# The last batch's output projection: weight sums and residual loads ahead, products between the small ones, results by one VectorE operation per 128 columns

## The chip, the cores and the metric

The kernel runs on one core of a Trainium2 chip, in one launch. The metric is the device time in microseconds; before the change three runs gave a median of 3935.7 (3933.7 to 3947.99).

## The reference

The input is 8 images of 512 channels and 32 x 32 = 1024 positions, in float32. Two layers follow, each an attention block on a normalised input with a residual. The change lies in the end of the second layer, of which this is the core (gn is a group norm without weights; the 4-d shapes are left out):

```python
def layer1(x, w_q, w_k, w_v, w_head, in_gamma, in_beta, w_proj, b_proj):
    n = gn(x)                                            # 8 x 512 x 1024
    q, k, v = (heads(w @ n) for w in (w_q, w_k, w_v))    # 8 heads of 64
    attn = einsum('bhdq,bhdT->bhqT', q, k) * 64 ** -0.5
    attn = einsum('gh,bhqT->bgqT', w_head, attn)         # mixes the heads
    attn = softmax(attn, axis=-1)
    mean, var = moments(attn, axes=(-2, -1))             # one pair for each head
    attn = (attn - mean) / sqrt(var + 1e-5) * in_gamma + in_beta
    out = einsum('bhqT,bhdT->bhqd', attn, v)
    out = out.reshape(b, 1024, 512)                      # mixes heads with tokens
    return x + (out @ w_proj.T + b_proj).transpose(0, 2, 1)
```

Since the mean of a softmax over its matrix is known, the normalisation of a head g is a scale A[g] and an offset; the offset goes through the sum of v, and through w_proj, to a constant for each output channel and head. The kernel writes `a.A` for the scales and `a.cv` for the offsets before the projection.

## The kernel before

Each image is worked on in turn; `b` counts them, and the last is b = 7. In the second layer, the order of every engine's instructions is the order of the program text (`tc.manual_schedule`): no planner moves anything. SyncE issues the large DMAs in the same order, and an issue that waits holds back those behind it.

For each image a loop over 8 blocks of queries (`p`) with 4 steps each forms scores (`scores`), brings them to ScalarE and by DMA into another grouping (`regroup`, tile `re`), mixes the heads (`mix`, exponentials on ScalarE), transposes on VectorE (`flip`), takes the moments (`moments`) and multiplies with v (`values`, `leave`). Two blocks make a chunk `n` of 128 channels of the attention's output, kept unnormalised in the tile `q` (`out_view`). `totals(n)` makes the row sums with small matmuls (L1780, L1782), takes their reciprocal (L1784), stores it (`zd`, L1790); `broadcast` loads it back spread over the partitions (`rzb`, L1802), and `divide(n)` multiplies the chunk by it (L1829). For the first three chunks these run in the course of the loop, on GpSimd; for the last chunk they come at the end, on SyncE's queue and VectorE.

In the first seven images the output projection takes seven products of half-size matrices. The last one has nothing behind it to overlap with, and goes its own way, in `out1_last`. It computes four output chunks `oc` of 128 channels, each from four input chunks `n` and in two halves `f` of 512 columns (a head owns 128 columns, so half f has the heads 4f to 4f + 3). `products(oc, blocks)` does the given input chunks of output chunk oc, and remembers which are done; chunks 0, 1 and 2 have a two-bank PSUM tile each, chunk 3 has two single banks, `halves`. A product of 512 columns in float32 shows as two matmul records in the trace. The scale A and the offset are applied to the product, not to the input: `instance` sums the squares (tile `isb`), `instance_end` multiplies with ones to add over the partitions (L1854), and works out A and cv with operations of 128 x 8, among them `rsqrt`. Four small matmuls (L1592) multiply cv with the sum of the weights over the input chunks (`wsum`, L1583 and L1585); with the bias they give `off`, which ScalarE adds to the residual x, 128 columns at a time (L1603). `check` counts row sums out of range, and `set_flag` turns that into a flag by a matmul (L1964); the flag is read at the program's end, and another path would run again if it were set.

At the end of the last image, the program's order is: the last `values`; `totals`, `broadcast` and `instance` of the last chunk; then `rest`. `rest` loads the residual, and then, for oc of 0 to 2, finishes the products of the input chunks 0 to 2 (chunk 0 is already complete in these, chunk 1 lacks one), with the weight sums, `instance_end`, `divide` and `check` behind oc 0, the small matmuls and ScalarE's additions behind oc 1, and the flag behind oc 2. After that come the products that need the divided chunk, all of chunk 3, and for each half a multiplication by A, an addition of the residual (L1623, L1628) and the store (L1629).

Of the kernel before, what the change touches and what calls it, by code (L numbers as in the profile page):

```python
# [9 lines left out]
F32 = mybir.dt.float32  # L10
I32 = mybir.dt.int32
AF = mybir.ActivationFunctionType
ALU = mybir.AluOpType
# [5 lines left out]
P = 128  # L19
# [448 lines left out]
def tile_two_attention_layers(  # L468
# [19 lines left out]
    nc = tc.nc  # L488
    B, C, T = x_d.shape
    H = w_head.shape[0]  # L490
    D = C // H
    NCC = C // P
    NT = T // P
    FB = 512
    NFB = T // FB
# [10 lines left out]
    def column(name, src):  # L506
        t = const.tile([P, src.shape[0] // P], F32, tag=name, name=name)
        nc.gpsimd.dma_start(out=t, in_=src.rearrange("(c p) -> p c", p=P))
        return t
# [13 lines left out]
    pb1 = column("pb1", b_proj)  # L523
# [142 lines left out]
    ys = const_tile("ys", [P, B, NCC])  # L666
# [34 lines left out]
    with ExitStack() as l0:  # L701
# [4 lines left out]
        zpool = l0.enter_context(tc.tile_pool(name="zpool", bufs=2))  # L706
# [572 lines left out]
    with ExitStack() as l1:  # L1279
# [5 lines left out]
        zpool = l1.enter_context(tc.tile_pool(name="zpool1", bufs=1))  # L1285
# [4 lines left out]
        NCH = NT // 2  # L1290

        def acc_psum(nm):
            return ps_a.tile([P, FB], F32, tag="a", name=nm)
# [10 lines left out]
        NF = 5  # L1304
        re_t = repool.tile([P, NF + 4, 2, FB], F32, tag="re", name="re")
# [62 lines left out]
        class Projection:  # L1368
# [10 lines left out]
            def products(self, m):  # L1379
                w = w_t[self.key]  # L1380
                left, right = {
                    1: (0, self.b11), 2: (1, self.b21), 3: (6, self.b22), 4: (2, self.t[:, 3]),
                    5: (3, self.t[:, 0]), 6: (4, self.t[:, 1]), 7: (5, self.t[:, 2]),
                }[m]
                if m == 2:
                    self.ps[2] = self.ps.pop(1)
                else:
                    self.ps[m] = m_psum(f"{self.nm}_{m}")
                for i in range(2):
                    for k in range(2):  # L1390
                        nc.tensor.matmul(  # L1391
                            self.ps[m][:, i], w[:, left, k * HC + i * P : k * HC + i * P + P],
                            right[:, k], start=(k == 0 and m != 2), stop=(k == 1),
                            skip_group_check=True,
                        )
# [114 lines left out]
        def out_view(b):  # L1510


            return qo_t[b].rearrange("p (n two) a t -> p n (two a t)", two=2)
# [36 lines left out]
        def out1_last(a):  # L1550


            b = a.b
            w = w_t["p", b]
            tiles, done = {}, set()

            def products(oc, blocks):
                blocks = [n for n in blocks if (oc, n) not in done]
                done.update((oc, n) for n in blocks)
                if oc not in tiles:  # L1560
                    tiles[oc] = m_psum(f"pp1_{b}_{oc}")
                for f in range(NFB):
                    for n in blocks:
                        nc.tensor.matmul(  # L1564
                            tiles[oc][:, f], w[:, n, ts(oc, P)], out_view(b)[:, n, ts(f, FB)],
                            start=(n == 0), stop=(n == NCH - 1),
                        )

            last = NCH - 1

            def rest():

                x = rawpool.tile([P, NCC, T], F32, tag="raw", name="xs_last")
                for oc in range(NCC):
                    nc.sync.dma_start(out=x[:, oc], in_=x1_d[b][ts(oc, P), :])
                wsum = epool.tile([P, 2 * T], F32, tag="e", name="wsum")[:, :C]
                ys = etpool.tile([P, NCC, NFB, FB], F32, tag="et", name="ys_last")
                small = acc_psum("small_last")
                off = stat.tile([P, NCC, H], F32, tag="off", name="off", bufs=1)
                for oc in range(3):  # L1580
                    products(oc, range(last))
                    if oc == 0:
                        nc.vector.tensor_add(wsum, w[:, 0], w[:, 1])  # L1583
                        for n in range(2, NCH):
                            nc.vector.tensor_add(wsum, wsum, w[:, n])  # L1585
                        a.instance_end(small)
                        a.divide(last)
                        a.check()
                    if oc == 1:
                        pc = small[:, H : H + NCC * H]  # L1590
                        for o in range(NCC):
                            nc.tensor.matmul(  # L1592
                                pc[:, o * H : o * H + H], wsum[:, ts(o, P)], a.cv,
                                start=True, stop=True,
                            )
                        nc.vector.tensor_add(
                            off, pc.rearrange("p (c g) -> p c g", g=H),
                            pb1.unsqueeze(2).to_broadcast([P, NCC, H]),
                        )
                        for o in range(NCC):  # L1600
                            for g in range(H):
                                xg = x[:, o, ts(g, P)]
                                nc.scalar.activation(  # L1603
                                    xg, xg, AF.Identity, bias=off[:, o, g : g + 1]
                                )
                set_flag(small)
                halves = [acc_psum(f"pp1_last_{f}") for f in range(NFB)]
                h = FB // P
                for oc in range(NCC):
                    if oc < last:  # L1610
                        products(oc, [last])
                    for f in range(NFB):
                        if oc < last:
                            ps = tiles[oc][:, f]
                        else:
                            ps = halves[f]
                            for n in range(NCH):
                                nc.tensor.matmul(  # L1618
                                    ps, w[:, n, ts(oc, P)], out_view(b)[:, n, ts(f, FB)],
                                    start=(n == 0), stop=(n == NCH - 1),  # L1620
                                )
                        y = ys[:, oc, f]
                        nc.vector.tensor_mul(  # L1623
                            y.rearrange("p (g t) -> p g t", t=P),
                            ps.rearrange("p (g t) -> p g t", t=P),
                            a.A[:, f * h : f * h + h].unsqueeze(2).to_broadcast([P, h, P]),
                        )
                        nc.vector.tensor_add(y, x[:, oc, ts(f, FB)], y)  # L1628
                        nc.sync.dma_start(out=out_d[b, ts(oc, P), ts(f, FB)], in_=y)  # L1629

            return products, rest

        class Attention1:
            def __init__(self, b):
# [169 lines left out]
                    in_=self.zd[t].rearrange("g i -> (g i)").partition_broadcast(D),  # L1804
                )

            def check(self):

                b = self.b
                zs = self.zs[:, :, :32]  # L1810
                junk = zpool.tile([P, T], F32, tag="rzb", name=f"junk_{b}")[
                    :64, : NCH * 32
                ].rearrange("p (n c) -> p n c", n=NCH)
                cnt = stat.tile([64, 2], F32, tag="cnt", name=f"cnt_{b}")
                nc.vector.tensor_scalar(
                    junk, zs, Z_MAX, 0.0, ALU.is_lt, ALU.add, accum_out=cnt[:, 0:1]
                )
                nc.vector.tensor_scalar(
                    junk, zs, 1.0 / RZ_MAX, 0.0, ALU.is_gt, ALU.add, accum_out=cnt[:, 1:2]
                )  # L1820
                nc.vector.tensor_add(cnt[:, 0:1], cnt[:, 0:1], cnt[:, 1:2])
                nc.vector.tensor_scalar(
                    chk[:64, 1, B * H + b : B * H + b + 1], cnt[:, 0:1],
                    -(2.0 ** 60), 2.0 ** 61 * NCH * 32, ALU.mult, ALU.add,
                )
# [151 lines left out]
        for b in range(B):  # L1977
            more = b + 1 < B
            a = Attention1(b)
# [32 lines left out]
            else:  # L2012
# [6 lines left out]
                out_products = []  # L2019
# [6 lines left out]
            last = NT - 1  # L2026
            a.sums(NCH - 1)
            if not more:
                a.values(last, 0, 2, 3)
                a.leave(last, 0)  # L2030
                out_products[0](0, [2])
                out_products[0](1, [0, 1])
                a.values(last, 1, 0, 1, 2, 3)
                a.leave(last, 1)
                a.totals(NCH - 1)
                a.broadcast(0)
                a.broadcast(1)
                a.instance()
                out_products[1]()
                continue  # L2040
# [83 lines left out]
```

## Time and profile before

| what | value |
|---|---|
| median of three runs | 3935.7 us (3933.7 to 3947.99) |
| the profiled execution: its time | 3948.04 us |
| its span, first to last instruction | 3946.2 us |
| mean granted TensorE clock | 0.998 |
| busy: TensorE (PE) | 3871.6 us, 98% |
| busy: VectorE (DVE) | 2736.6 us, 69% |
| busy: ScalarE (ACT) | 1966.8 us, 50% |
| last `values` matmul ends, by the chain | 3913.44 us |
| last product record ends, by the chain | 3939.83 us |
| last VectorE result ends | 3941.34 us |

A line of the timeline has the start in us from the span's start, the length, the engine, the line of the code, the operation, what it writes and reads with shapes, how many instructions are merged in it, and in brackets how long the engine idled before it and for what. The chain of waits goes back from the last instruction, at each step to what released it. DVE is VectorE, ACT is ScalarE, PE is TensorE, PEld its weight loads, SPq SyncE's queue.

### The profile page before, as it was taken

To read this page: it belongs to the slowest core of one execution; us is meant where nothing else is said; L and a number is where in the kernel's file an instruction comes from. 1 tells how busy PE (TensorE), PEld (TensorE's weight loads), DVE (VectorE), ACT (ScalarE), POOL (GpSimd) and SP (SyncE) were. 2 spreads that over 40 slices of the span, in tenths; PEclk is the share of its full clock that TensorE was granted. 3 is DMA by queue.
4 is the path that set the end of the run, shared out by engine and by line. 5 is a ranking of instruction groups with operands and counts; after the bars stand their busy time and mean duration, and the time that the engine had idled before them with its cause. 6 is when DMAs were issued, how large, how long until landed. Compare 5 with 4: busy or idle time off the path is not lost. (4 is left out here: it accounts for less than half of the span.)

```text
span 3946.2 us, 95344 instructions
## 1 busy us (share of the span) xinstructions
PE 3871.6 (98%) x41868; PEld 1822.3 (46%) x41868; DVE 2736.6 (69%) x3713; ACT 1966.8 (50%) x2400; POOL 207.4 (5%) x210
## 2 busy tenths in 40 slices
PE   8999999999999999999999999999999999999998
PEld 4353535344353535344554544545545545445454
DVE  4747476665758474756867958859768678678597
ACT  1726354453627172534725717528447257176275
POOL 0000000000000000000110100201101102002010
PEclk9999999999999999999999999999999999999999
DMA  3313131212121121216947839749559479297395
GB/s 120 120 53 116 49 116 43 84 35 77 55 75 66 64 73 52 87 46 168 221 135 190 230 97 229 191 128 239 167 149 228 142 177 223 97 227 204 114 228 146
DMA packets 249593, 519.09 MB, mean 132 GB/s; under 512 B 51024, under 2 KB 58192, under 8 KB 242512
## 3 DMA queue, kind: packets, MB, share of 16 engines
q1 hardware_dynamic: 241984, 500.08, 44.7%
q0 software_dynamic: 7184, 12.81, 1.6%
q8 instruction: 331, 5.42, 0.6%
q14 instruction: 94, 0.77, 0.1%
HBM read 197.16 MB, written 46.92 MB: 62 GB/s over the span
## 5 line engine op out<-in xcount | busy, mean ns | idle before, releaser
L1712 DVE STREAM_TRANSPOSE et<-e 128x2048 f32<-128x2048 f32 x256 | 589.5, 2303 | 133.5 <-ACT e L1697 132.5
L1742 PEld LDWEIGHTS a<-et,v 128*64 128x64 f32 x16384 | 506.4, 138 | 294.0 <-issue 268.5
L1726 DVE BATCH_NORM_STATS2 bn<-e 128x6 f32<-128x512 f32 x1024 | 635.0, 680 | 0.0
L1093 ACT ACTIVATE e<-s 128x1024 f32<-128x1024 f32 x512 | 497.1, 1026 | 232.8 <-PE s L1088 232.7
L1659 ACT COPY raw<-s 128x1024 f32<-128x1024 f32 x480 | 470.2, 1018 | 218.9 <-PE s L1647 192.5
L1697 ACT ACTIVATE e<-m 128x1024 f32<-128x1024 f32 x512 | 496.2, 1021 | 157.4 <-PE m L1684 55.1
L1742 PE MATMUL a<-et,v 128*64 128x64 f32 x16384 | 554.7, 224 | 8.7 <-issue 6.2
L1103 DVE TENSOR_TENSOR zacc<-zacc,e 128x1024 f32<-128x1024 f32 x384 | 468.8, 1221 | 124.6 <-ACT e L1093 100.5
L1647 PE MATMUL s<-k,q 64*64 64x512 f32 x4096 | 515.6, 606 | 6.9 <-DVE q L1506 3.2
L1088 PE MATMUL s<-q,k 64*64 64x512 f32 x4096 | 490.3, 594 | 2.3 <-ACT e L1093 2.3
L1116 PE MATMUL a<-e,v 64*64 64x512 f32 x4096 | 484.1, 589 | 0.0
L1684 PE MATMUL m<-re,wmix 32*32 32x512 f32 x8192 | 312.8, 599 | 17.8 <-DMA re<-raw 14.4
L1116 PEld LDWEIGHTS a<-e,v 64*64 64x64 f32 x4096 | 156.6, 133 | 282.8 <-issue 282.3
L1088 PEld LDWEIGHTS s<-q,k 64*64 64x64 f32 x4096 | 146.4, 133 | 284.2 <-issue 217.8
L1647 PEld LDWEIGHTS s<-k,q 64*64 64x64 f32 x4096 | 128.0, 132 | 222.5 <-issue 90.5
L1790 POOL DMA_DIRECT2D zd<-rz x96 | 52.3, 550 | 3390.0 <-DMA y<-x 1868.5
L1466 PE MATMUL pv<-wv,y 128*128 128x512 f32 x480 | 216.0, 603 | 0.0
L1758 ACT COPY q<-a 64x256 f32<-64x256 f32 x256 | 93.8, 367 | 136.4 <-PE a L1742 134.5
L1466 PEld LDWEIGHTS pv<-wv,y 128*128 128x128 f32 x480 | 89.3, 191 | 120.9 <-issue 107.5
L1684 PEld LDWEIGHTS m<-re,wmix 32*32 32x32 f32 x8192 | 69.3, 103 | 163.2 <-ACT raw L1659 71.7
L1472 DVE COPY v<-pv 128x512 f32<-128x512 f32 x30 | 20.7, 690 | 159.7 <-ACT v L1472 80.3
L906 PE MATMUL pv_p<-left_v,tmp 128*128 128x256 f32 x512 | 115.0, 380 | 3.3 <-DVE tmp L935 3.3
(318 smaller groups left out, 3859.5 us busy)
## 6 DMA issues: line engine op xcount, KB each, us to landing
re<-raw SPq DMA_DIRECT2D x1024, 256.0 KB
left_q<-left_q SPq DMA_DIRECT2D x17, 1792.0 KB
left_p<-left_p SPq DMA_DIRECT2D x17, 1792.0 KB
left_k<-left_k SPq DMA_DIRECT2D x10, 1792.0 KB
x<-in_x_dram SPq DMA_DIRECT2D x32, 512.0 KB
rzb<-zd SPq DMA_DIRECT2D x128, 128.0 KB
x<-x SPq DMA_DIRECT2D x64, 256.0 KB
y<-x SPq DMA_DIRECT2D x32, 512.0 KB
```

Source lines behind the costliest of these rows:

```text
L1088: nc.tensor.matmul(ps[c * D : c * D + D, m], k[r, hp, k0 : k0 + D], q[r, hp, ts(f, FB)], start=True, stop=True,)
L1093: nc.scalar.activation(e[i], ps, AF.Exp, scale=S0 * S0)
L1103: nc.vector.tensor_add(zacc[g], zacc[g], e[i])
L1116: nc.tensor.matmul(acc[g][a][m * D : m * D + D], v[rows, kc, ts(2 * hp + m, D)], e[i][rows, m], start=(kc == 0), stop=(kc == NG - 1),)
L1466: nc.tensor.matmul(ps[:, m], y_t[b][:, c, ts(2 * i + m, P)], w[:, c], start=(c == 0), stop=(c == NCC - 1),)
L1647: nc.tensor.matmul(ps[c * D : c * D + D, m], qo_t[b][r, p, hp, ts(c, D)], k_t[b][r, hp, ts(kh, FB)], start=True, stop=True,)
L1659: nc.scalar.copy(dst, ps)
L1684: nc.tensor.matmul(ps[a // 2][c * 32 : c * 32 + 32, a % 2].rearrange("p (r h k) -> p h r k", r=2, h=2), wmix[rows].rearrange("p g i -> p ( ...
L1697: nc.scalar.activation(e[:, :, 2 * h : 2 * h + 2].rearrange("p r a k -> p a r k"), ps[h].rearrange("p a (r k) -> p a r k", r=2), AF.Exp,)
L1712: nc.vector.transpose(self.et[p, u].rearrange("p kb (r st a) g q -> p st kb r (a g q)", r=2, st=2)[:, st], self.e[p, s].rearrange("p r a ( ...
L1726: nc.vector.bn_stats(self.bn[n][:, p % 2, s, a], e[:, :, a].rearrange("p r k -> p k r"))
L1742: nc.tensor.matmul(acc[two * D : two * D + D, s].rearrange("p (x q) -> p x q", q=4), v_t[b][:, kb, ts(g, D)], et[:, kb, :, g], start=(kb = ...
```

## The change

- The residual loads and the weight sums move out of `rest` into a new function `inputs`. It is called before the last `values` of the last query block: the loads go to SyncE's queue ahead of `zd` and `rzb`, the sums to VectorE ahead of the row sums' reciprocal.
- The missing products of chunk 1 go before the `isb` matmul, and those of chunk 2 between it and the small matmuls. Half 0 of chunk 3 is begun (three of its four input chunks) before the flag's matmul.
- `check` comes directly behind `instance_end`, and writes what it has no use for to a free part of the tile `re`, no longer to the buffer of `rzb`. `divide` comes behind `off`, and the 32 additions of ScalarE are written behind `set_flag`.
- The multiplication and the addition on 512 columns (two operations) become four operations on 128 columns, each with one column of A as its scalar.

```diff
-            def rest():
+            kept = []
+
+            def inputs():
                 x = rawpool.tile([P, NCC, T], F32, tag="raw", name="xs_last")
                 for oc in range(NCC):
                     nc.sync.dma_start(out=x[:, oc], in_=x1_d[b][ts(oc, P), :])
                 wsum = epool.tile([P, 2 * T], F32, tag="e", name="wsum")[:, :C]
+                nc.vector.tensor_add(wsum, w[:, 0], w[:, 1])
+                for n in range(2, NCH):
+                    nc.vector.tensor_add(wsum, wsum, w[:, n])
+                kept.extend((x, wsum))
+
+            def rest():
+                x, wsum = kept
                 ...
-                for oc in range(3):
-                    products(oc, range(last))
-                    if oc == 0:
-                        nc.vector.tensor_add(wsum, w[:, 0], w[:, 1])
-                        for n in range(2, NCH):
-                            nc.vector.tensor_add(wsum, wsum, w[:, n])
-                        a.instance_end(small)
-                        a.divide(last)
-                        a.check()
-                    if oc == 1:
-                        pc = small[:, H : H + NCC * H]
                 ...
+                products(1, range(last))
+                a.instance_end(small)
+                a.check(re_t[:64, NF + 3, 1, : NCH * 32])
+                products(2, range(last))
+                pc = small[:, H : H + NCC * H]
+                for o in range(NCC):
+                    nc.tensor.matmul(
+                        pc[:, o * H : o * H + H], wsum[:, ts(o, P)], a.cv,
+                        start=True, stop=True,
+                    )
+                nc.vector.tensor_add(
+                    off, pc.rearrange("p (c g) -> p c g", g=H),
+                    pb1.unsqueeze(2).to_broadcast([P, NCC, H]),
+                )
+                halves = []
+
+                def half(f, blocks):
+                    if f == len(halves):
+                        halves.append(acc_psum(f"pp1_last_{f}"))
+                    for n in blocks:
+                        nc.tensor.matmul(
+                            halves[f], w[:, n, ts(last, P)], out_view(b)[:, n, ts(f, FB)],
+                            start=(n == 0), stop=(n == NCH - 1),
+                        )
+
+                half(0, range(last))
+                a.divide(last)
                 set_flag(small)
+                for o in range(NCC):
+                    for g in range(H):
+                        xg = x[:, o, ts(g, P)]
+                        nc.scalar.activation(
+                            xg, xg, AF.Identity, bias=off[:, o, g : g + 1]
+                        )
                 ...
                         else:
+                            half(f, [last] if f == 0 else range(NCH))
                             ps = halves[f]
                 ...
-                        y = ys[:, oc, f]
-                        nc.vector.tensor_mul(
-                            y.rearrange("p (g t) -> p g t", t=P),
-                            ps.rearrange("p (g t) -> p g t", t=P),
-                            a.A[:, f * h : f * h + h].unsqueeze(2).to_broadcast([P, h, P]),
-                        )
-                        nc.vector.tensor_add(y, x[:, oc, ts(f, FB)], y)
-                        nc.sync.dma_start(out=out_d[b, ts(oc, P), ts(f, FB)], in_=y)
+                        for i in range(h):
+                            g = f * h + i
+                            nc.vector.scalar_tensor_tensor(
+                                ys[:, oc, f, ts(i, P)], ps[:, ts(i, P)], a.A[:, g : g + 1],
+                                x[:, oc, ts(g, P)], ALU.mult, ALU.add,
+                            )
+                        nc.sync.dma_start(out=out_d[b, ts(oc, P), ts(f, FB)], in_=ys[:, oc, f])
 ...
                 a.leave(last, 0)
                 out_products[0](0, [2])
                 out_products[0](1, [0, 1])
+                out_products[2]()
                 a.values(last, 1, 0, 1, 2, 3)
```

More of the change, by code (lines that the diff above doesn't have):

```diff
@@ L1579, in rest @@
                 off = stat.tile([P, NCC, H], F32, tag="off", name="off", bufs=1)
-                for oc in range(3):
-                    products(oc, range(last))
-                    if oc == 0:
-                        nc.vector.tensor_add(wsum, w[:, 0], w[:, 1])
-                        for n in range(2, NCH):
-                            nc.vector.tensor_add(wsum, wsum, w[:, n])
-                        a.instance_end(small)
-                        a.divide(last)
-                        a.check()
-                    if oc == 1:
-                        pc = small[:, H : H + NCC * H]
[L1591 to L1594, printed above, removed]
-                            )
-                        nc.vector.tensor_add(
-                            off, pc.rearrange("p (c g) -> p c g", g=H),
-                            pb1.unsqueeze(2).to_broadcast([P, NCC, H]),
-                        )
[L1600 to L1605, printed above, removed]
@@ L1606, in rest @@
-                set_flag(small)
-                halves = [acc_psum(f"pp1_last_{f}") for f in range(NFB)]
+                products(1, range(last))
[8 more added lines that the diff above has]
+                    )
@@ L1615, in rest @@
                         else:
+                            half(f, [last] if f == 0 else range(NCH))
                             ps = halves[f]
[L1617 to L1621, printed above, removed]
-                        y = ys[:, oc, f]
-                        nc.vector.tensor_mul(
-                            y.rearrange("p (g t) -> p g t", t=P),
-                            ps.rearrange("p (g t) -> p g t", t=P),
-                            a.A[:, f * h : f * h + h].unsqueeze(2).to_broadcast([P, h, P]),
-                        )
-                        nc.vector.tensor_add(y, x[:, oc, ts(f, FB)], y)
-                        nc.sync.dma_start(out=out_d[b, ts(oc, P), ts(f, FB)], in_=y)
-            return products, rest
+                        for i in range(h):
[5 more added lines that the diff above has]
+                        nc.sync.dma_start(out=out_d[b, ts(oc, P), ts(f, FB)], in_=ys[:, oc, f])
+            return products, rest, inputs
         class Attention1:
@@ L1805, in broadcast, with check @@
                 )
-            def check(self):
+            def check(self, place=None):
                 b = self.b
                 zs = self.zs[:, :, :32]
-                junk = zpool.tile([P, T], F32, tag="rzb", name=f"junk_{b}")[
-                    :64, : NCH * 32
-                ].rearrange("p (n c) -> p n c", n=NCH)
+                if place is None:
+                    place = zpool.tile([P, T], F32, tag="rzb", name=f"junk_{b}")[:64, : NCH * 32]
+                junk = place.rearrange("p (n c) -> p n c", n=NCH)
                 cnt = stat.tile([64, 2], F32, tag="cnt", name=f"cnt_{b}")
```

## The prediction

> **What bounds the kernel now.** The page comes first: TensorE (PE) is busy 98% of 3946.2 us, and the granted clock is full almost throughout. The edit touches only the end of the eighth batch, so I then read the chain that ended last, restricted to its last 47 us (columns: start, length, what).
>
> ```profile
> 3913.58 0.31 PE z L1782 x4
> ...
> 3916.19 0.69 DVE wsum L1583
> ...
> 3917.62 0.69 DVE wsum L1585
> 3918.31 0.09 DVE ivar L1856
> ...
> 3921.04 0.18 DVE icv L1866
> ...
> 3921.27 1.06 PE small_last L1592 x8
> 3922.32 5.25 PE pp L1564 x12
> 3927.58 0.12 PE small_last L1964 x2
> 3927.69 5.26 PE pp L1564 x12
> 3932.95 6.88 PE pp_last L1618 x16
> ...
> 3940.65 0.69 DVE ys_last L1628
> ```
>
> Two stretches set the end. From 3913.89 to 3921.27 it is VectorE: the row sums, then three weight sums (`wsum`), then the sixteen tiny operations from `ivar` to `icv`. From 3921.27 to 3939.83 it is TensorE without a hole, 40 matmul records of the output product at 5.25/12 = 0.4375 us each, plus 1.06 and 0.12. One pair of VectorE operations and the last transfer follow: `ys_last` ends at 3941.34 and the span 4.86 later.
>
> The timeline of the same stretch shows what surrounds that chain.
>
> ```profile
> 3913.91 0.35 DVE L1784 RECIPROCAL rz<-z 64x32 f32<-64x32 f32 x1 [2.73 <-PE z L1782]
> ...
> 3916.41 0.36 PE L1854 MATMUL small_last<-isb,ones 64*128 64x8 f32 x2 [2.54 <-DVE isb L1845]
> ...
> 3916.70 3.32 PE L1564 MATMUL pp<-q,left_p 128*128 128x512 f32 x4
> ...
> 3925.52 9.46 ACT L1603 ACTIVATE xs_last<-xs_last,off 128x128 f32<-128x128 f32 x32 [11.29 <-DVE off L1596]
> ```
>
> VectorE idles 2.73 us just before the row sums, TensorE 2.54 us just after them, and then TensorE does only four records before it needs `icv`. It is short of ready work in the front half and has too much in the back half.
>
> **The change, part by part.** All sums are against the profiled execution: span 3946.2, time 3948.04. Its time is 12.3 us above the median shown, 3935.7; I take the same difference off the median.
>
> *Weight sums ahead.* The three operations take 2.12 us (3916.19 to 3918.31) and now follow `sq`, which ends at 3911.17. They end near 3913.3, inside the 2.73 us idle, 0.6 before the row sums arrive; without that idle they would cost up to 2.12. `ivar` then starts when its own matmul is done, about 3916.8 instead of 3918.23, and `icv` ends near 3919.8.
>
> *Residual loads ahead.* Four SyncE (SP) issues (0.42 to 0.58 us each) of 512 KB. They move past the four `zd` stores and two `rzb` broadcasts, behind the last regrouping transfers, whose issues end at 3889.4. The queue then has nothing until 3914.29, so they delay no issue. DMA is saturated until about 3892.3, then idle; 2 MB at the 270 GB/s moved there is about 8 us, so they land near 3901. They can only slow the tail of the regrouping, whose last consumer, the `mix` at 3898.79, has over 6 us in hand; I take 0 and bound it at 0 to 1 us. In return the broadcasts no longer share the DMA with them; `divide` waited until 3923.09 for these.
>
> *TensorE order.* Before the `isb` matmul stand four records of chunk 1: 3913.89 + 1.75 = 3915.64, done before `isb` (3916.27). The `isb` matmul starts at 3916.41 as before, and at 3916.70 the twelve records of chunk 2 follow: 3921.95. `icv` has been ready for 2 us, so the 1.06 us of small products ends at 3923.01. Six records of the last chunk's first half: 3925.64. The flag matmul needs VectorE: `off` at 3923.06 (0.17), `divide` (1.22), then the five flag operations (0.73, from the rows L1958 to L1963), so `good` is there near 3925.2, 0.4 early; behind the flag matmul's wait all remaining products queue, so a late `rzb` would count in full. Flag 0.12: 3925.76. Twelve records that needed `divide`: 3931.01. Two for half 0: 3931.89. Eight for half 1: 3935.39. Before, this point was 3939.83: 4.44 earlier. As a balance: twelve records (5.25) leave the stretch behind the small products, and those end 0.69 later.
>
> *The clock.* The 3.32 us for four records is not their price: the granted clock fell to half. Windows of 3.4 us (columns: length, PE busy with count, clock, DMA share, GB/s):
>
> ```profile
> 1896.50:1899.90 3.40, 0.95 (x34) 1.00 0.96 239
> 1899.90:1903.30 3.40, 3.34 (x24) 0.50 1.05 250
> ...
> 3913.80:3917.20 3.40, 0.86 (x5) 1.00 0.06 2
> 3917.20:3920.60 3.40, 2.82 (x4) 0.50 0.43 99
> ```
>
> The Trainium skill (TensorE: Matmul & The Clock Gate, Why this matters for your kernels) asks only that idle gaps stay below about 3 us. Here a gap of 2.54 us was enough, since it lay in one window; the measurement decides. Before, the slow clock cost nothing, as `icv` came after the four records anyway. After the change the same place has no such cover. In a window of the same phase TensorE would be busy 0.1 + 1.75 + 0.79 = 2.6 us, with one gap of about 0.8. Both windows above dropped below 1 us; one other drop, at 1800.9, followed 1.79 us, so 2.6 is clear but not by much. By rule and by row there is no drop, but the margin comes from the row alone. A drop would add half a window, 1.7 us.
>
> *One VectorE operation per 128 columns.* Removed: 16 operations of 0.69 us, 1.39 per 512 columns (the start of one L1623 to the next). Added: 32 of a shape that the trace lacks. The nearest rows have the same operation, at 512 and 64 columns:
>
> ```profile
> 92.24 1.41 DVE L962 SCALAR_TENSOR_TENSOR q<-pq_p,qkvb,tmp 128x512 f32<-128x512 f32 x2 [0.69 <-PE pq_p L906]
> ...
> L1770 DVE SCALAR_TENSOR_TENSOR sq<-bn 128x64 f32<-128x64 f32 x32 | 7.9, 248 | 1.1
> ```
>
> Two at 512 take 1.41, one 0.75, so the second starts 0.66 to 0.67 after the first. A column is (1.22 - 0.69)/512 = 1.04 ns (additions of 1024 and 512 columns), so 384 fewer leave 0.35 long and 0.27 apart. From 64 columns up it is 0.31 long, 0.23 apart. I take 0.27, since that row reads PSUM as the new operation does. Against it stands the Trainium skill (VectorE: DVE Perf Modes, The DRAIN you can't avoid): the next operation does not start until the pipe is empty, and only one that is not held starts earlier. For held operations that makes 0.35 apart. The row shows an overlap of 0.08 for the same operation from PSUM; I follow the row.
>
> VectorE: chunk 0 is complete in PSUM at 3925.76 + 1.75 = 3927.51. 28 pieces at 0.27 end at 3935.1, before half 1 is ready at 3935.39; then 0.05 + 3 x 0.27 + 0.35 end at 3936.6. At 0.35 VectorE is the bound: 3927.55 + 32 x 0.35 = 3938.75. With the old pairs, 3927.55 + 8 x 1.39 = 3938.7: the fusion is needed to keep the last 2 us.
>
> ScalarE: its 32 additions start with `off` near 3923.3 and take 9.46, so end near 3932.8. The first piece is used at 3927.55, with 14 in hand, and the 32nd near 3936; never late. Output: 256 KB each 1.08 us is 243 GB/s; the DMA moved 349 GB/s at a share of 0.92 earlier in this tail, so no backlog; bound 0 to 0.8.
>
> **Sum.** 3941.34 - 3936.6 = 4.7 us off; span 3941.5, time 3943.3 in that execution, 3931.0 against the median: 0.12% less.
>
> **Rivals.**
> *VectorE becomes the bound* (0.35 apart): end 3938.75, 2.6 us off, 3933.1. For it: the skill's rule, and a PSUM source. Against: the 0.67 above.
> *A slow-clock window* at 3917 or later: 1.7 less gain, 3932.7. For it: this very place lost its clock. Against: 2.6 busy of 3.4.
> *The early loads or the broadcasts do harm*, and the gain goes: 0 to 2 us off, 3934.7. For it: DMA at its ceiling until 3892. Against: 6 us in hand, and a less busy DMA at 3918.
> *The other side: each piece is held by its wait on ScalarE.* Now 32 operations each wait for a semaphore. If each first let its forerunner finish and then paid the 0.10 us that separate L1623 from the dependent L1628, the pitch would be 0.45: end 3927.55 + 14.4 = 3941.95, 0.6 us slower, 3936.3. It decides from (3941.34 - 3927.55)/32 = 0.431. Against: L1623 at 3932.72 waits for TensorE and still starts 0.07 before its forerunner ends.
>
> **How the numbers follow.** Likeliest 0.65, VectorE bound 0.15, slow clock 0.09, early loads 0.07, held pieces 0.04. The mechanisms alone span 3930 to 3936.5. But the three runs of the kernel before lie between 3933.7 and 3947.99 and the profiled one is at 3948.04, so a median of few runs can come out 12 us higher with nothing changed: 3931 + 12 = 3943. So 3928 to 3944. About 0.5% (19.7 us) is what a measurement of this kernel can tell from no change; no case reaches it either way, nor does that spread with the gain added (17). I leave 0.03 for faster, 0.95 for within, 0.02 for slower.
>
> **What would show it.** Right: `wsum` before the row sums; `small_last<-icv` not waiting for VectorE, near 3923; the slow clock after the row sums gone; new pieces of 0.31 to 0.35 us, 0.23 to 0.27 apart; TensorE's last record near 3935.4 and 6 us from there to the span's end. Wrong: pieces further apart than 0.28, so that VectorE ends later than 1.2 us after TensorE; a wait of the flag matmul; a `mix` near 3895 that waits for its regrouping; or a change upstream of 3889, where the program is the same.

## The result and the profile after

The changed kernel takes 3930.62 us (median of 22 runs, 3927.36 to 3944.06), the kernel before 3940.76 (22 runs beside them, 3931.73 to 3948.85). The ratio is 0.9982, 95% interval 0.9975 to 0.9989: 7.1 us less (4.3 to 9.8); the means lie 7.4 us apart, the medians 10.1. The forecast was 3931.0, 4.7 us less, and no change by the bound of 0.5%. The time and the class are as forecast; the gain came out larger than the sum. A second comparison gave 0.9972 (0.9962 to 0.9982), some 11 us less.

The profiled execution has a span of 3932.8 us. It can't be set against the 3946.2 of before directly: the last `values` record ends at 3904.51 here and at 3913.44 before, though the program up to there is the same but for the moved loads and weight sums. From here on, times with a plus sign count from the end of that record. They leave the scatter of everything ahead of it out.

These are lines of the timeline after, in the same columns as those of before (start, length, engine, line, operation, output and inputs, count, idle time ahead of it):

```profile
3902.18 0.69 DVE L1579 TENSOR_TENSOR wsum<-left_p 128x512 f32<-128x512 f32 x1
...
3904.88 1.98 PE L1564 MATMUL pp<-q,left_p 128*128 128x512 f32 x4
3904.98 0.35 DVE L1795 RECIPROCAL rz<-z 64x32 f32<-64x32 f32 x1 [0.66 <-PE z L1793]
...
3907.48 0.36 PE L1865 MATMUL small_last<-isb,ones 64*128 64x8 f32 x2 [0.62 <-DVE isb L1856]
3907.77 5.42 PE L1564 MATMUL pp<-q,left_p 128*128 128x512 f32 x12
...
3910.69 0.17 DVE L1877 TENSOR_TENSOR icv<-icv,vs 128x8 f32<-128x8 f32 x1
...
3913.02 0.95 PE L1596 MATMUL small_last<-icv,wsum 128*128 128x8 f32 x8
...
3914.38 1.22 DVE L1840 TENSOR_TENSOR q<-q,rzb 128x1024 f32<-128x1024 f32 x1 [0.18 <-DMA rzb<-zd]
...
3918.71 6.29 DVE L1636 SCALAR_TENSOR_TENSOR ys_last<-pp,iA,xs_last 128x128 f32<-128x128 f32 x24 [1.56 <-PE pp L1564]
...
3921.86 4.46 PE L1610 MATMUL pp_last<-q,left_p 128*128 128x512 f32 x10
...
3926.43 1.13 DVE L1636 SCALAR_TENSOR_TENSOR ys_last<-pp_last,iA,xs_last 128x128 f32<-128x128 f32 x4 [0.39 <-PEq L2083]
```

VectorE's idle 2.73 us ahead of the row sums is down to 0.66, since `wsum` stands in it. TensorE's 2.54 us ahead of `isb` is down to 0.62. `icv` is ready at 3910.86, 2.2 us before the small products read it. Between 3907.48 and the last product record at 3926.32 TensorE has no hole.

| from the end of the last `values` record | before | forecast | after |
|---|---|---|---|
| small products begin | +7.83 | +8.51 | +8.51 |
| last product record ends | +26.4 | +21.95 | +21.8 |
| last VectorE result ends | +27.9 | +23.2 | +23.0 |
| span ends | +32.8 | +28.0 | +28.3 |

So within the two profiled executions the tail is 4.5 to 4.9 us shorter, and the sum of the prediction holds to 0.3 us at each point. What it does not explain is why the runs show 7 us, and in the second comparison 11. The experiments were made for that, and for what each part of the change is worth.

### The profile page after: what moved, and what is told of

Its sections match the earlier page's. It is cut to its first block, busy times and chain, and to the rows that moved or that the text cites. A ratio compares the mean times of both kernels' runs of the same rounds, so it can differ in the third digit from the quotient of the medians.

```text
span 3932.8 us, 95352 instructions
## 1 busy us (share of the span) xinstructions
PE 3867.3 (98%) x41868; PEld 1821.3 (46%) x41868; DVE 2735.0 (70%) x3729; ACT 1968.2 (50%) x2400; POOL 207.4 (5%) x210
```

## The experiments

The theory: TensorE's order gives the products an earlier end, and the quicker results let VectorE follow. Rivals: one part alone does it; the weight sums or loads ahead are the gain; or the clock, which fell to half in the tail before, is part of it. Here are the readings of all profiles, each from its own timeline, with the drops of the clock between the last `values` record and the last product record (place, length).

| kernel | products end | last result | half clock in the tail |
|---|---|---|---|
| before, first profile | +26.4 | +27.9 | +3.8, 3.4 us |
| before, second | +28.8 | +30.4 | +2.6, 10.2 us |
| before, third | +28.1 | +29.6 | +8.9, 3.4 us |
| before, only the 128-column results | +29.8 | +31.0 | +4.5, 10.2 us |
| before, idle time filled | +26.4 | +28.0 | none |
| after, old order of products | +26.7 | +27.9 | +8.2, 3.4 us |
| after, old pairs of operations | +22.1 | +26.0 | none |
| after, weight sums late | +22.1 | +23.3 | none |
| after, loads late | +21.8 | +23.0 | none |
| after, first and second profile | +21.8, +21.8 | +23.0, +23.0 | none |
| more ahead, first form | +22.8 | +23.6 | none |
| more ahead, second form, twice | +21.2, +21.2 | +21.9, +21.9 | none |

### The old pairs in the new order

In this cut the arguments are shortened.

```diff
-                        for i in range(h):
-                            g = f * h + i
-                            nc.vector.scalar_tensor_tensor(ys[:, oc, f, ts(i, P)], ...)
+                        nc.vector.tensor_mul(y, ps, A)
+                        nc.vector.tensor_add(y, x[:, oc, ts(f, FB)], y)
```

> The changed kernel with the old multiplication and addition of 512 columns in place of the operations of 128. Times from the end of the last values record (before: last product record +26.4, last result +27.9, span +32.8; after: +21.8, +23.0, +28.3). If VectorE has to be quicker for the earlier products to pay: it starts at +14.2 as after and takes eight pairs of 1.39, so the last result is at +25.3, 2.3 later than after, with the products still at +21.8. If TensorE alone sets the end: last result at +23.3.

Ratio to before 0.999 (0.9983 to 0.9997). Three lines of its timeline:

```profile
3915.59 1.23 DVE L1841 TENSOR_TENSOR q<-q,rzb 128x1024 f32<-128x1024 f32 x1 [0.55 <-DMA rzb<-zd]
...
3922.33 0.69 DVE L1640 TENSOR_TENSOR ys_last<-xs_last,ys_last 128x512 f32<-128x512 f32 x1 [0.47 <-ACT xs_last L1621]
...
3930.68 0.69 DVE L1640 TENSOR_TENSOR ys_last<-xs_last,ys_last 128x512 f32<-128x512 f32 x1
```

The products end at +22.1, the results at +26.0, 3.9 us behind them: VectorE sets the end without the new operations. The other reading, TensorE alone sets the end, put it at +23.3, and is out. The loss of 3.0 against after is larger than the 2.3 expected, by a wait of 0.47 for ScalarE, and by `divide`, which in this execution got its broadcast 0.4 us later (3915.59 is +10.25, against +9.87 after) and so held back the flag's matmul.

### The 128-column results alone

The edit is that of the change, in the kernel before.

> The kernel before with nothing but the operations of 128 columns. If TensorE set the end before: products still at +26.4, last result at +27.6, 0.3 us earlier, and the ratio within 0.05% of 1. If the quicker results are where the gain comes from: last result before +26. A ratio well below 0.9995 with the tail 0.3 us shorter would mean that times differ for a cause outside the tail.

Ratio 1.0 (0.9991 to 1.0008). The results end 1.24 us after the last product record instead of 1.52, so 0.3 us is gained, as expected. But the products themselves end at +29.8 instead of +26.4, with the same order of TensorE's work as before:

```profile
3914.41 1.87 PE L1592 MATMUL small_last<-icv,wsum 128*128 128x8 f32 x8 [2.03 <-DVE icv L1865]
3916.14 7.99 PE L1564 MATMUL pp<-q,left_p 128*128 128x512 f32 x12
```

Twelve records take 7.99 us, in the first profile of before 5.40. The clock was at half for 10.2 us and covers the small products and much of these. So a drop of the clock in the old order need not be hidden, as it was in the profile on which the forecast stood.

### The old order of the products, all else as after

```diff
-                products(1, range(last))
+                products(0, range(last))
                 a.instance_end(small)
+                products(1, range(last))
                 a.check(re_t[:64, NF + 3, 1, : NCH * 32])
-                products(2, range(last))
+                a.divide(last)
                 ...
+                products(2, range(last))
-                half(0, range(last))
-                a.divide(last)
                 set_flag(small)
                 ...
-                            half(f, [last] if f == 0 else range(NCH))
+                            half(f, range(NCH))
```

Chunk 0 was complete before, so its line does nothing.

> The changed kernel with weight sums and loads ahead and operations of 128, but the products in the old order around the small ones. If the order is the larger part: cv is ready at +6.4, the small products end at +7.4, 40 records of 0.4375 and the flag follow, so the products end at +25.0 and the last result is at +26.3; the weight sums alone are worth 1.3. The clock may drop after the idle 2.5 us, without cost. If the weight sums are the larger part: products at +22 to +23.

Ratio 0.9989 (0.9983 to 0.9996). Lines of its timeline:

```profile
3908.14 0.36 PE L1865 MATMUL small_last<-isb,ones 64*128 64x8 f32 x2 [2.54 <-DVE isb L1856]
...
3911.57 1.06 PE L1597 MATMUL small_last<-icv,wsum 128*128 128x8 f32 x8 [1.17 <-DVE icv L1877]
...
3912.49 7.09 PE L1564 MATMUL pp<-q,left_p 128*128 128x512 f32 x12
```

`icv` at +6.35 and the small products as expected; then the twelve records took 7.09 instead of 5.4 us. The expected +25.0 and half of a 3.4 us drop give +26.7, which is what was measured. I had expected the drop "without cost"; that was wrong. The weight sums ahead do not stand in for the order.

The runs say the same less sharply. The old order keeps 4.3 us (1.6 to 6.7) of gain, while its tail ends only 1.4 us ahead of the mean of three profiles of the kernel before (+27.9 against +29.3). Its median is 3937.85, against 3930.62 and 3931.53 of the changed kernel and 3936.92 with the old pairs; beside these the kernel before had 3940.76 to 3941.77. So both the order and the new results are needed, but what each is worth in us is read from the profiles.

### Weight sums late, loads late

The three additions, and in the other kernel the four loads, move from `inputs` back into `rest`.

```diff
                 products(1, range(last))
+                nc.vector.tensor_add(wsum, w[:, 0], w[:, 1])
+                for n in range(2, NCH):
+                    nc.vector.tensor_add(wsum, wsum, w[:, n])
                 a.instance_end(small)
```

```diff
                 x, wsum = kept
+                for oc in range(NCC):
+                    nc.sync.dma_start(out=x[:, oc], in_=x1_d[b][ts(oc, P), :])
```

> The changed kernel with the three weight sums back behind the row sums, ahead of ivar. If the new order of the products covers them: ivar and cv come 1.5 us later, at +7.9 instead of +6.4, still before the twelve records of chunk 2 end at +8.5, so the products end at +21.8 and nothing is lost. If the weight sums ahead are a gain of their own: products at +23.3.

> The changed kernel with the residual loads back behind the broadcasts. If the early loads only took traffic off the broadcasts: divide comes 0 to 0.6 us later (it started at +9.9 after), the flag's matmul waits for what of it exceeds 0.2, products at +21.8 to +22.3. If the additions of ScalarE needed the loads early: they wait for a load after off, and results come 1 to 3 us later.

There is one run of each, profiled, so no ratio. Weight sums late:

```profile
3905.49 0.17 DVE L1877 TENSOR_TENSOR icv<-icv,vs 128x8 f32<-128x8 f32 x1
...
3906.40 0.95 PE L1596 MATMUL small_last<-icv,wsum 128*128 128x8 f32 x8
...
3908.12 1.23 DVE L1840 TENSOR_TENSOR q<-q,rzb 128x1024 f32<-128x1024 f32 x1 [0.54 <-ACT xs_last L1621]
```

`icv` ends at +7.8 instead of +6.35, and the small products start at +8.51, unmoved. The products end 0.3 later, but not for the weight sums: `divide` started at +10.23, as in the run with the old pairs, and VectorE stood idle for 0.54 us ahead of it. So in the new order, moving the weight sums ahead is worth nothing in this profile.

Loads late gives the same end as after, to 0.02 us:

```profile
3906.71 1.12 SPq L1813 DMA_DIRECT2D rzb<-zd  x2
3907.89 2.00 SPq L1586 DMA_DIRECT2D xs_last<-x  x4
...
3911.59 1.23 DVE L1840 TENSOR_TENSOR q<-q,rzb 128x1024 f32<-128x1024 f32 x1
```

The loads follow the broadcasts at once, at +6.0 (the changed kernel issues them at -25.1, so it is the queue's order alone that holds them), and `divide` starts at +9.68, not later than with the loads far ahead (+9.6 to +10.25). Here neither the broadcasts nor ScalarE needed them early.

### The kernel before with its idle time filled, and twice more as it was

Three products into a bank that is overwritten later, before the `isb` matmul and again before the small products:

```diff
+                tiles[2] = m_psum(f"pp1_{b}_2")
+                def fill():
+                    for n in range(3):
+                        nc.tensor.matmul(
+                            tiles[2][:, 0], w[:, n, ts(2, P)], out_view(b)[:, n, ts(0, FB)],
+                            start=True, stop=True,
+                        )
+                fill()
                 for oc in range(3):
                     products(oc, range(last))
+                    if oc == 1:
+                        fill()
```

> The kernel before with six more products of 512 columns (12 records), thrown away: three in TensorE's idle time before the isb matmul, three behind the four records that precede the small products. Nothing else differs. If the half clock costs the kernel before time in most executions (3.4 us of it in the profile of the operations of 128 alone, none in the first profile): no drop of the clock in the tail, last product record at +26.3 to +26.7, and over many runs 1 to 3 us faster than before (ratio 0.9993 to 0.9998). If the clock is no part of it: same time, or slower by what the products delay the isb matmul (0.1 to 0.3 us).

> The kernel before once more, for the place of the clock's drop. If the drop falls at random against the tail: between 0.5 and 10 us after the last values record, and the last product record between +26.4 and +29.8, the later the more of the 40 records it covers. If the first profile is typical: drop at +3.8, last record at +26.4.

> The kernel before a third time; as for the second: drop at random and the last product record between +26.4 and +29.8, or drop at +3.8 and the last record at +26.4.

The second profile of before, in TensorE's windows (length, busy and count, granted clock, DMA share, GB/s):

```profile
3918.50:3921.92 3.42, 1.24 (x34) 1.00 0.02 1
3921.92:3925.33 3.41, 3.05 (x5) 0.50 0.06 2
3925.33:3928.74 3.41, 2.82 (x10) 0.50 0.92 175
3928.74:3932.15 3.41, 3.41 (x6) 0.50 0.97 368
```

and two lines of its timeline:

```profile
3927.14 1.88 PE L1592 MATMUL small_last<-icv,wsum 128*128 128x8 f32 x8 [0.59 <-DVE icv L1866]
3928.88 7.02 PE L1564 MATMUL pp<-q,left_p 128*128 128x512 f32 x12
```

The drop lasts three windows here, and runs on past the arrival of `icv`; the products end at +28.8. In the third profile it comes later, at +8.9, and takes half of 3.4 us: +28.1.

```profile
3906.05:3909.46 3.41, 1.05 (x9) 1.00 0.85 144
3909.46:3912.87 3.41, 3.41 (x6) 0.50 0.93 336
```

With the idle time filled, nothing drops, though TensorE does 12 records more:

```profile
3911.10 2.84 PE L1584 MATMUL pp<-q,left_p 128*128 128x512 f32 x6
...
3916.01 2.74 PE L1584 MATMUL pp<-q,left_p 128*128 128x512 f32 x6
...
3919.49 5.40 PE L1564 MATMUL pp<-q,left_p 128*128 128x512 f32 x12
```

The twelve records take 5.40 and the products end at +26.4. So the idle time causes the drop, and the drop costs the old order up to 3.4 us. In the runs this version is at 0.9995 (0.9988 to 1.0002): in the expected direction, but the interval holds 1, so the runs alone would not show it.

### More ahead

After the change TensorE still has a hole of 0.62 us, and four results follow its last record. The first form put four records of chunk 2 before the `isb` matmul and the whole flag before the small products, and split the last half in two pieces of 256 columns.

> The changed kernel with four more records (chunk 2, first block) before the isb matmul, the flag before the small products, and the last half in two pieces of 256 columns with two results and a store each. If TensorE sets the end: its hole of 0.62 before the isb matmul is gone and two results fewer follow its last record, so the last result is at +22.0, 1.0 earlier than after, span at +27.1. If VectorE is by now as much the bound: last result at +22.5 or later.

Ratio 0.9984 (0.9974 to 0.9993); the last result at +23.6, 0.5 later than after. Its timeline says why:

```profile
3909.28 0.28 DVE L1871 TENSOR_REDUCE isb<-re 64x8 f32<-64x128 f32 x1
3910.73 0.39 PE L1880 MATMUL small_last<-isb,ones 64*128 64x8 f32 x2
...
3915.73 0.38 PE L1990 MATMUL small_last<-good,ones 128*128 128x1 f32 x2 [0.99 <-DVE good L1989]
```

Four records are too much for the hole: `isb` was ready at 3909.56 and its matmul came at 3910.73. All of VectorE's chain moved back with it, and the flag's matmul, now earlier, waited 0.99 us for that chain. The second form takes one product (two records), and leaves the flag's matmul where the change has it, with VectorE's five flag operations ahead of `off`:

```diff
                 products(1, range(last))
+                nc.tensor.matmul(tiles[2][:, 0], w[:, 0, ts(2, P)],
+                                 out_view(b)[:, 0, ts(0, FB)], start=True, stop=False)
                 a.instance_end(small)
                 a.check(re_t[:64, NF + 3, 1, : NCH * 32])
+                good = flag_ready()
                 ...
+                for e in range(2):
+                    at = slice(e * FB // 2, (e + 1) * FB // 2)
+                    for n in range(NCH):
+                        nc.tensor.matmul(ends[e][:, at], w[:, n, ts(last, P)],
+                                         out_view(b)[:, n, FB + at.start : FB + at.stop], ...)
+                    results(last, 1, ends[e], range(2 * e, 2 * e + 2))
```

> The changed kernel with two records (one product of chunk 2) in the hole before the isb matmul, VectorE's five flag operations ahead of off and divide with the flag's matmul where it was, and the last half in two pieces as in the version before. If TensorE's hole and the two last results were 0.6 and 0.3 of the end: last product record at +21.4, last result at +22.1, span at +27.2, 0.9 to 1.0 earlier than after. If the arrival of the broadcast now decides (divide at +9.9 to +10.3, products that need it from +11.1): last result at +22.4 to +22.8.

> The version with the hole filled by two records, the flag operations ahead and the last half in two pieces, once more. In the trace: last result at +21.9 to +22.2, span at +27.3 to +27.5, about 1 us before the changed kernel's. In the runs: 1 us is 0.03%, so its ratio is expected at 0.9977 to 0.9987 and not to be told from the changed kernel's; if the two pieces cost something outside the tail, its ratio is above 0.999.

```profile
3908.33 1.02 PE L1592 MATMUL pp<-q,left_p 128*128 128x512 f32 x2
...
3909.29 0.39 PE L1890 MATMUL small_last<-isb,ones 64*128 64x8 f32 x2
...
3923.70 3.62 PE L1660 MATMUL pp_last<-q,left_p 128*128 128x256 f32 x16
...
3925.90 2.15 DVE L1640 SCALAR_TENSOR_TENSOR ys_last<-pp_last,iA,xs_last 128x128 f32<-128x128 f32 x8
```

The hole is gone, and the last result ends at +21.9 in both profiles, 1.15 us before the changed kernel's; the span ends at +27.3 and +27.6, against +28.3 and +27.9. In the runs it is at 0.9991 (0.9983 to 1.0) and 0.998 (0.9973 to 0.9987) of before. The changed kernel, beside the second of these:

> The changed kernel once more, beside the next one on the same chip. If the tail and the clock are the whole of the gain: no drop of the clock before the last product record, that record at +21.8 to +22.1 and the last result at +23.0 to +23.4, and about 6 us faster than before over many runs (ratio 0.998 to 0.999). If part of the first ratio came from elsewhere: ratio above 0.999 with the same tail.

It was at 0.9972 (0.9962 to 0.9982), lower than the 0.998 to 0.999 expected, without a drop in the tail, and with the last result again at +23.0. So the second form is better by 1 us in the trace, and the runs do not show it: the intervals overlap, with the changed kernel's on the lower side.

## Why the prediction was right, and where not

**The order of the products** was right to 0.2 us: small products at +8.5, the last record at +21.8. Undone alone, it puts the last record back to +26.7, of which 1.7 is clock; the other 3.2 are the order itself.

**The results per 128 columns.** The row taken (the same operation at 512 columns, from PSUM) gave 0.35 long and 0.27 apart; measured 0.34 long and (6.29 - 0.34)/23 = 0.26 apart. The rival that VectorE becomes the bound, and the one in which each piece is held by its wait on ScalarE, both fall: every piece waits for a semaphore of ScalarE and still starts 0.08 before its forerunner ends. That the fusion is needed was right in kind and too small in size: 3.0 us, not 2.

**The weight sums ahead** were booked with no gain of their own, beyond an earlier `icv`; the run shows that this earlier `icv` isn't needed.

**The loads ahead.** That they would relieve the broadcasts is not borne out, at no cost: `divide` starts at +9.6 to +10.8 in the six profiles with the loads late, and at +9.6 to +10.25 in seven with them early (in the eighth, the first form of more ahead, VectorE itself came later). That the regrouping isn't harmed was right as far as the profiles tell: the last `mix` that waits for it waits 0 to 0.9 us with the loads late and 0 to 1.7 with them early, 0.5 and 0.8 on average; a cost of a few tenths is not excluded. The remark that a late broadcast counts was right, less a margin of some 0.1 us (0.4 was forecast): with `divide` at +10.23 and +10.25 instead of +9.87, the products end 0.3 later.

**The clock** is the term that was mis-sized. "Before, the slow clock cost nothing" is true of the one profile that I had. In two more profiles of the same kernel the products end 1.7 and 2.4 us later for it, in the one with only the new results 3.4. The mean of the three profiles of before is +29.3 for the last result, against +23.0 after: 6.2 us, instead of the 4.7 forecast. Three profiles are few, and the second of them is the slowest execution on record, 3956.57 us. The margin against a new drop was thin, too: the prediction counted on 2.6 us busy in a window, where 0.86 to 1.79 had preceded drops, and the old order lost its clock after 2.24. The rest of the mechanism stands: in the eight profiles that have the new order the clock is full up to the last product record.

What stays open: 6.2 us lies inside the first interval (4.3 to 9.8) and just outside the second (about 7 to 15). The end of the last `values` record scatters between 3897.9 and 3919.3 over the 14 profiles of all kernels. Nearly all of this stands there long before the change: the last `flip` of the image before the last starts between 3624.7 and 3643.0 us, and from there to the end of the last `values` record every profile takes 273.1 to 276.4 us. No instruction that the change touches has run by then. In the five profiles of kernels without `inputs` this `flip` starts at 3635.8 us on average, in the nine with it at 3630.5. The cause of these 5 us, chance or not, is not shown; they may be what the runs hold beyond the tail. The wide range of the forecast, drawn for that scatter, was needed only in part: the median fell within 1 us of its likeliest value. That is closer than the sum deserves: it was made from 3935.7, and over more runs the kernel before has 3940.76, so a smaller gain from a lower start gave the same end.

## What to carry to other kernels

Where small dependent operations interrupt the matmuls, put independent matmul work between them until the wait is just covered: two records filled a hole of 0.62 us, four delayed the chain behind it. An idle stretch there was paid twice in this kernel, once as idle time and once as half clock on what follows, and a single profile happened to hide the second payment; profile the same kernel more than once before booking it at nothing. When TensorE ends earlier, look at once at the engine that follows: without shorter results 3.0 of the 4.9 us between the two first profiles would have stayed in VectorE's queue.

## What the runs showed of the hardware

Gaps of 2.54 us, with a second one of 0.6 to 2.6 us behind them, brought a drop of the granted clock to 0.50 in each of the five profiles that had them, and gaps of 0.62 us in none of five. In three of the five the drop began ahead of the second gap. In the third profile of before and in the old order it followed the window with the second gap, 2.59 and 1.17 us long. This is the old order:

```profile
3909.93:3913.34 3.41, 2.24 (x12) 1.00 0.52 143
3913.34:3916.75 3.41, 3.41 (x5) 0.50 0.06 11
```

The Trainium skill (TensorE: Matmul & The Clock Gate, Why this matters for your kernels) asks only for no idle gaps above about 3 us, and by that none of the five would have lost time; they lost 0 to 3.4 us, and the measurement decides.

The place of the drop against the tail differs in each execution (+2.6 to +8.9), and so does its length, 3.41 or 10.24 us, one or three windows. What ends it was not settled. In the first profile a window with 2.82 us busy was followed by full speed; in the second the ones with 3.05 and 2.82 were not. In the kernel with only the 128-column results not even a full window was:

```profile
3914.53:3917.95 3.42, 3.42 (x10) 0.50 0.79 253
3917.95:3921.36 3.41, 3.41 (x5) 0.50 0.88 357
3921.36:3924.80 3.44, 3.44 (x11) 1.00 0.08 33
```
